# Sharing one buffer between the stages of a four-layer network, with image 1's norm inside image 0's heads and image 0's sampling positions in two halves

## The chip, the cores and the metric

The kernel runs on one NeuronCore of one Trainium2 chip, as one program. Its time is the device time of one execution in microseconds; the median of three runs is given. Everything is float32. TensorE is called PE here, its weight loads PEld, VectorE DVE, ScalarE ACT, GpSimd POOL; SP is the engine that issues most of the direct DMAs.

## The reference

Four images of 32 x 32 pixels and 384 channels go through four layers. Each layer is pre-normed (a group norm with 32 groups of 12 channels) and added back to its input.

```python
# layer 0: deformable attention, 6 groups = 6 heads of 64 channels
q = x @ w_q + b_q
o = conv3x3(q, w_off0, groups=6) + b_off0
o = gelu(layernorm(o) * ln_g + ln_b)
pos = tanh(o_group @ w_offp) * 16 + pixel              # one (x, y) per pixel and group
xs = bilinear_sample(x_group, pos)                     # four neighbours, weighted
k, v = xs @ w_k + b_k, xs @ w_v + b_v
bias = bilinear_sample(rpe_group, (pixel - pos) / 2)   # 1024 x 1024 a head
out = softmax(q k^T / 8 + bias) v;  x = x + out @ w_out + b_out

# layer 1: 12 heads of 32 channels
xg = x @ Wg + bg;  gc = depthwise_conv3x3_stride2(xg)
sim = sigmoid(l2norm(xg) l2norm(gc)^T);  gw = gamma * (sim sim^T) + 1 - gamma
attn = softmax(q k^T * scale) * gw;  attn = attn / attn.sum(queries);  x = x + (attn v) @ Wproj

# layer 2: local sums of x and x^2 over 5 columns and 20 channels, and their quotient
# layer 3: outlook attention, a 3 x 3 neighbourhood, weights from x @ Wa, values x @ Wv
```

## The kernel before

`Net` holds what is shared and two lanes. `Front` is layer 0 (tiles on the right side of SBUF), `Trunk` is layers 1 to 3 (tiles on the left). The Tile framework places tiles, decides a static order of instructions for each engine and inserts the waits; a few places are pinned in the order in which they are written. Engines and DMA queues work in order.

**Order of the whole.** The front of image 0 runs alone. From then on `Net.layer3` steps the trunk of image b as a generator; each step yields a weight, and the front of image b+1 is advanced by its own weights so that it stays a tenth ahead (TRUNK_STEPS 1109, FRONT_STEPS 714, LEAD 0.1). Image 3's trunk has no front beside it.

**PSUM.** `big` is a ring of two tiles of 128 x 1024, `bank` a ring of four of 128 x 512. The weights pool has three buffers.

**Front.** `inputs0` (L533) loads the image, transposes it (L545, copies by ACT), stores it to `x0`, norms it (statistics L306 and L307, group sums on PE L330, scaling L357), transposes the normed image back (L564) and writes it to memory in pairs of neighbouring pixels (L570), two DMAs for each of eight pixel blocks. Then come q (a `dense_t`, L376), the grouped convolution (L599), the layer norm (L628 to L650) and GELU (L654), and `positions` (L451), which makes sampling weights, the gather indices `sidx` (L509), and the bias windows' indices and fractions. For each of eight pixel blocks `gather` (L667) issues six indirect DMAs from POOL into one of three `gat` buffers, and `weigh` (L680 to L683) reduces it on DVE; a transpose (L694) and k and v follow.

**Heads of image 0.** `heads0` (L819) runs 96 blocks (6 heads x 2 halves of queries x 8 key blocks) in a pinned order, one block a turn. A block's bias window is gathered five blocks early (`win`, 8 buffers); ACT and DVE interpolate it in two steps each (`z`, 5 buffers, ACT L904 and DVE L885; then `lg`, 23 buffers, DVE L890), AHEAD = 8 turns before the block's logits are added (L935). Maximum, subtraction (L954), exponential and the products with v follow in later turns. Other images use `head0`, which does the same work (L752 to L808) as part of the front's steps.

**Trunk, layer 1.** `inputs1` (L1059) loads `x1`, norms it into another tile, multiplies by Wg, takes the stride-2 convolution on DVE (L1088, L1090), then `queries_keys` (L1096): for each of three channel blocks the q and k products go to a `big` tile each and to memory (`qd`, `kd`), from where `load_sums` and `load_pair` fetch them by head. `sums_step` (L1237), eight for each pair of heads, takes both `big` tiles: products (L1246), maxima (L1254) and exponentials with their sums (L1255). `hall` (L1158) spreads the inverse norms through a `big` tile and a bank. `sims` (L1276) makes the sigmoids (L1285, L1292). Then six `pair`s of heads: L1350, L1365, L1395, L1403 and L1404 are their group weights and products.

**Layer 3.** L1660 and L1662 write the outlook weights to memory and load them back as masks `mt`, half from the SP queue and half from the ACT queue; eight transposes of x (L1671) go to eight `y` tiles (L1675), L1683 multiplies masks and values, and each block is added and written out (L1692).

Of the kernel before, what the change touches and what calls it, by code (L numbers as in the profile page):

```python
# [19 lines left out]
I32 = mybir.dt.int32  # L20
# [52 lines left out]
class Net:  # L73


    def __init__(self, ctx, tc, a):
        self.tc, self.nc, self.a = tc, tc.nc, a
        nc = self.nc
        pool = lambda name, bufs, **kw: ctx.enter_context(
            tc.tile_pool(name=name, bufs=bufs, **kw)  # L80
        )
        self.const = pool("const", 1)
        self.wts = pool("wts", 3)
        self.ps2 = pool("ps2", 2, space=PSUM)
        self.ps1 = pool("ps1", 4, space=PSUM)
        self.dram = pool("dram", 1, space=DRAM)
        self.n = 0
        self.consts()
        self.scratch()
        self.front, self.trunk = Front(self, "right"), Trunk(self, "left")  # L90

# [102 lines left out]
    def scratch(self):  # L194
# [11 lines left out]

        self.k0 = dram("k0", [C, N])
# [72 lines left out]
class Lane:  # L280
# [33 lines left out]
    def norm(self, x, out, mv=None):  # L314


        nc = self.nc
# [4 lines left out]
        gmat = self.weights("gmat")  # L322
# [3 lines left out]
        def groups(src):  # L326
# [13 lines left out]
        nc.vector.tensor_scalar(mean, groups(mv[:, :, 0:1]), 1.0 / 12.0, None, ALU.mult)  # L340
# [8 lines left out]
        nc.scalar.activation(  # L349
            rstd, groups(d), AF.Sqrt, bias=self.eps[:, 0:1], scale=1.0 / 12.0  # L350
        )
        nc.vector.reciprocal(rstd, rstd)
        for k in range(KC):
            src = x[:, k, :]
            if len(out.shape) == 4:
                src = src.rearrange("p (y x) -> p y x", y=HW)
            nc.vector.tensor_scalar(  # L357
                out[:, k],
                src,
                mean[:, k : k + 1],  # L360
                rstd[:, k : k + 1],
                ALU.subtract,
                ALU.mult,
            )
# [34 lines left out]
class Front(Lane):  # L399
# [51 lines left out]
    def positions(self, oall):  # L451

        nc, v = self.nc, self.nc.vector
        NC = NJ * G
        tmp = self.wt([P, NC, GC], "a12", 2)
        og = oall.rearrange("p j (g c) -> p (j g) c", g=G)
        th = self.wt([P, 2, NC], "ix_th")
        for t in range(2):
# [6 lines left out]
        v.scalar_tensor_tensor(  # L465
            pos.rearrange("p t (j g) -> p (t j) g", g=G),
            th.rearrange("p t (j g) -> p (t j) g", g=G),
            HW / 2.0,
            bc(self.ref.rearrange("p t j -> p (t j)"), 2, G),
            ALU.mult,  # L470
            ALU.add,
        )
# [25 lines left out]
        w4 = self.wt([P, NC, 2, 2], "w4", 1)  # L498
        for lr in range(2):
            v.tensor_tensor(w4[:, :, lr, 0], wx[:, lr, :], one[:, 1, :], ALU.mult)  # L500
            v.tensor_tensor(w4[:, :, lr, 1], wx[:, lr, :], al[:, 1, :], ALU.mult)
        fi = self.wt([P, NJ, G], "ix_fi")
        fi2 = fi.rearrange("p j g -> p (j g)")
        sidx = self.wt([P, NC], "sidx", 1, I32)

        def index(out, hi, lo, mul, which):
            v.scalar_tensor_tensor(fi2, hi, float(mul), lo, ALU.mult, ALU.add)
            v.tensor_tensor(fi, fi, bc(self.gofs[:, which, :], 1, NJ), ALU.add)
            v.tensor_copy(out, fi2)  # L509

        index(sidx, fl[:, 1, :], fl[:, 0, :], HW, 0)
# [7 lines left out]
        f = self.f  # L519
# [7 lines left out]
        index(self.widx[:, 0], fl[:, 1, :], fl[:, 0, :], WROW, 1)  # L527

        v.tensor_scalar(fi2, fi2, float(HW // 2 * WROW), None, ALU.add)
        v.tensor_copy(self.widx[:, 1], fi2)  # L530
        return w4, sidx

    def inputs0(self, b):  # L533
        nc, v = self.nc, self.nc.vector
        pairs = self.pairs[b % 2]

        xin = self.wt([P, NJ, C], "a12", 2)
# [3 lines left out]
        x = self.wt([P, KC, N], "a12", 2)  # L541
        for j in range(NJ):
            ps = self.bank()
            for k in range(KC):
                nc.tensor.transpose(  # L545
                    ps[:, k * P : (k + 1) * P], xin[:, j, k * P : (k + 1) * P], self.ident
                )
            nc.scalar.copy(
                x[:, :, j * P : (j + 1) * P], ps[:, 0:C].rearrange("p (k n) -> p k n", k=KC)
            )  # L550
        nc.scalar.dma_start(self.x0[b % 2].rearrange("(k p) n -> p k n", p=P), x)
        xh = self.wt([P, KC, N], "a12", 2)
        self.norm(x, xh)
# [6 lines left out]
        pv = pairs.rearrange("(g s) (y c) -> y s g c", g=G, y=2)  # L560
        for j in range(NJ):
            ps = self.bank()
            for k in range(KC):
                nc.tensor.transpose(  # L564
                    ps[:, k * P : (k + 1) * P], xh[:, k, j * P : (j + 1) * P], self.ident
                )
            xn = self.wt([P, C], "xn", 2)
            nc.scalar.copy(xn, ps[:, 0:C])
            for y, first in ((0, HW + 1), (1, 1)):
# [3 lines left out]
                )  # L573

        yield 10
# [50 lines left out]
        for j in range(NJ):  # L626
            st = self.wt([P, 6], "ln_st", 2)
            v.bn_stats(st, oall[:, j, :])  # L628
            v.bn_aggr(mv[:, j, :], st)
        rstd = self.wt([P, NJ], "ln_rstd")  # L630
        nc.scalar.activation(
            rstd,
            mv[:, :, 1:2].rearrange("p j o -> p (j o)"),
            AF.Sqrt,
            bias=self.eps[:, 1:2],
        )
        v.reciprocal(rstd, rstd)
        for j in range(NJ):
            v.tensor_scalar(
                oall[:, j, :],  # L640
                oall[:, j, :],
                mv[:, j, 0:1],
                rstd[:, j : j + 1],
                ALU.subtract,
                ALU.mult,
            )
            v.tensor_tensor(
                oall[:, j, :], oall[:, j, :], self.rows[:, R_LNG : R_LNG + C], ALU.mult
            )
            v.tensor_tensor(  # L650
                oall[:, j, :], oall[:, j, :], self.rows[:, R_LNB : R_LNB + C], ALU.add
            )
        for j in range(NJ):
            nc.scalar.activation(oall[:, j, :], oall[:, j, :], AF.Gelu)  # L654
        yield 25
        w4, sidx = self.positions(oall)
        yield 20
# [161 lines left out]
    def heads0(self, work):  # L819
# [10 lines left out]
        AHEAD, SUB, OUT = 8, 10, 11  # L830
# [12 lines left out]
        def divide(step, k):  # L843
# [6 lines left out]
            elif step == 1:  # L850
# [3 lines left out]
                for q in range(2):  # L854
                    inv[q] = tile_of([P, HN], "lg", 23)
# [11 lines left out]
        def turn(t):  # L867
            i = t + AHEAD

            if i + 5 < n:  # L870
                h, q, j = blocks[i + 5]
                win[i + 5] = tile_of([P, (HH + 1) * WROW], "win", 8)
# [20 lines left out]
            if 0 <= i < n:  # L893
                lg[i] = tile_of([P, HN], "lg", 23)
# [6 lines left out]
            if 0 <= i + 1 < n:  # L901
                wv = win[i + 1].rearrange("p (r c) -> p r c", c=WROW)
                z[i + 1] = tile_of([P, HH, HW + 1], "z", 5)
# [88 lines left out]
        for i in range(4):  # L992
            h, q, j = blocks[i]
            win[i] = tile_of([P, (HH + 1) * WROW], "win", 8)
# [12 lines left out]
        self.load_keys(1)  # L1007
        for t in range(-3, n + OUT + 12):
            turn(t)
        yield 0  # L1010
# [25 lines left out]
class Trunk(Lane):  # L1036


    def image(self, b, out):
        with self.scope("l1y"):  # L1040
# [18 lines left out]
    def inputs1(self, b):  # L1059
        nc, v = self.nc, self.nc.vector  # L1060
        x = self.wt([P, KC, N], "x")
        for k in range(KC):
            nc.sync.dma_start(x[:, k, :], self.x1[b % 2][k * P : (k + 1) * P, :])
        xh = self.wt([P, KC, N], "xh")
        self.norm(x, xh)
        yield 15

# [28 lines left out]
        def queries_keys(ko):  # L1096
            for w, dst in ((wq, self.qd), (wk, self.kd)):
                ps = self.dense_t(w, xh, ko)
                t = self.wt([P, N], "qk", 2)
                if dst is self.qd:  # L1100
                    nc.scalar.mul(t, ps, HD1**-0.5)
                else:
                    v.tensor_copy(t, ps)
                nc.sync.dma_start(dst[ko * P : (ko + 1) * P, :], t)
# [9 lines left out]
        queries_keys(0)  # L1114
# [25 lines left out]
        queries_keys(1)  # L1140
        yield 14
        wv = self.weights("Wqkv", 2 * C)
# [4 lines left out]
        queries_keys(2)  # L1147
        yield 14
        self.sums_step(1, st)
        yield 10  # L1150
        values(range(NJ // 2))
        self.sums_step(2, st)
        yield 18
        for k in range(KC):
            rows, heads = slice(k * P, (k + 1) * P), slice(32 * k, 32 * k + 32)
            ps, pc = self.big(), self.bank()
            for out, lo in ((ps[:, 0:512], 0), (ps[:, 512:N], 512), (pc[:, 0:M1], N)):
                nc.tensor.matmul(  # L1158
                    out,
                    self.hall[heads, :],  # L1160
                    inv[heads, lo : lo + out.shape[-1]],
                    start=True,
                    stop=True,
                )
            t = self.wt([P, N + M1], "sq", 2)
            v.tensor_tensor(
                t[:, 0:N].rearrange("p (y x) -> p y x", y=HW),
                pads[k][:, 1:, 1:],
                ps.rearrange("p (y x) -> p y x", y=HW),
                ALU.mult,  # L1170
            )
            v.tensor_tensor(t[:, N:], raw[:, k, :], pc[:, 0:M1], ALU.mult)
# [4 lines left out]
            self.sums_step(3 + k, st)  # L1177
            yield 8
        for i in range(2):
            values(range(4 + 2 * i, 6 + 2 * i))  # L1180
            self.sums_step(6 + i, st)
        self.sums_finish(0, st)
        self.load_lse(0)
        yield 28
# [91 lines left out]
    def sims(self, p):  # L1276

        nc = self.nc
        sim = self.wt([P, 2, 2, N], "sim")
# [148 lines left out]
    def layers23(self, b, out):  # L1428
        with self.scope("l23"):
            self.x = self.wt([P, KC, N], "x")  # L1430
# [36 lines left out]
    def layer2(self):  # L1467
        nc, v = self.nc, self.nc.vector
        with self.scope("l2"):
# [8 lines left out]
            def squares(k):  # L1478
# [24 lines left out]
                d = self.wt([P, HW, HW], "d", KC)  # L1503
# [61 lines left out]
    def layer3(self, b, out):  # L1565
        nc, v = self.nc, self.nc.vector
        skew = self.skew[b % 2]
        with self.scope("l3"):
# [98 lines left out]
            ys = []  # L1667
            for i in range(NJ):
# [5 lines left out]
                y = self.wt([P, C], "y", NJ)  # L1674
                nc.scalar.copy(y, pt[:, 0:C])  # L1675
                ys.append(y)
            yield 20
            for i in range(NJ):
# [11 lines left out]
                y = ys[i]  # L1690
# [87 lines left out]
```

## Time and profile before

| | us |
|---|---|
| runs | 4781.11, 4804.75, 4805.06; median 4804.75 |
| profiled execution | 4803.82 |
| its span | 4802.0 |
| busy PE / DVE / ACT / POOL | 4201.4 / 3136.5 / 2411.3 / 942.6 |
| front 0 up to its k and v | 0 to 219 |
| heads of image 0 | 219 to 548 |
| trunk 0 with front 1 | from 574 |
| trunk 3 alone | 4030 to 4802 |

All times in the profile are microseconds from the start of the span. A row of the timeline gives start, duration, engine, source line, operation, destination and sources, shapes and count; in brackets stands the engine's idle time before it and what released it. A row of the groups gives busy time and mean ns of one, then the idle time before. In the lines of 40 digits, a digit is a busy share, or the granted TensorE clock, in tenths of one fortieth of the span. Float32 matmuls appear as two records each.

### The profile page before, as it was taken

The numbers are of one execution on the slowest core, as the hardware profiler recorded it, in microseconds if no ns is written. First come the engines' busy times: TensorE is split into PE (matmuls) and PEld (weight loads), VectorE is DVE, ScalarE is ACT, GpSimd is POOL, SyncE is SP. The second block draws the span as 40 slices with busy tenths as digits, with TensorE's granted clock in tenths as the row PEclk, the third lists the DMA queues.
The fourth block names the chain that finished last, engine by engine and source line by source line (L and its number), as shares of the span: only waits on it lengthen the run. The fifth ranks groups of instructions, "written<-read, shape, count | busy, mean of one in ns | idle before, by whom it ended". The sixth has DMA issues, their size and how long they took to land. (4 is left out here: it accounts for less than half of the span.)

```text
span 4802.0 us, 46610 instructions
## 1 busy us (share of the span) xinstructions
PE 4201.4 (87%) x15704; PEld 1793.1 (37%) x15704; DVE 3136.5 (65%) x5727; ACT 2411.3 (50%) x3693; POOL 942.6 (20%) x946
## 2 busy tenths in 40 slices
PE   5477798999999898899999989799999998999988
PEld 2222243333333353333333444343333334343444
DVE  3599655777877727577778744667686873455544
ACT  2166333666665313566767332456676631466642
POOL 0643104211212102311212110421121210000000
PEclk8689897999999987999999989799999998899998
DMA  6433234222212233321212133431121213201011
GB/s 118 142 102 103 81 101 131 84 60 57 71 40 73 75 116 123 106 57 48 80 50 68 44 100 116 130 98 55 38 77 39 79 47 109 86 25 31 19 39 40
DMA packets 230927, 366.82 MB, mean 76 GB/s; under 512 B 117475, under 2 KB 164672, under 8 KB 230688
## 3 DMA queue, kind: packets, MB, share of 16 engines
q1 hardware_dynamic: 169672, 197.36, 13.9%
q0 software_dynamic: 39936, 145.53, 10.3%
q10 hardware_dynamic: 21080, 20.96, 1.8%
q8 instruction: 124, 2.03, 0.2%
q14 instruction: 115, 0.94, 0.1%
HBM read 285.84 MB, written 78.21 MB: 76 GB/s over the span
## 5 line engine op out<-in xcount | busy, mean ns | idle before, releaser
L1404 DVE SCALAR_TENSOR_TENSOR e<-bank,gam,e 128x512 f32<-128x512 f32 x768 | 558.3, 749 | 571.8 <-ACT gn L1403 276.4
L1395 PE MATMUL bank<-sim,sg 128*128 128x512 f32 (+3 forms) x2304 | 877.4, 515 | 11.6 <-POOL sg L1350 8.9
L1255 ACT ACTIVATE big<-big,nmax 128x1024 f32<-128x1024 f32 x384 | 418.6, 1090 | 395.2 <-DVE nmax L1254 340.2
L1373 ACT ACTIVATE e<-big 128x1024 f32<-128x1024 f32 x384 | 376.9, 1019 | 363.4 <-PE big L1365 358.1
L1395 PEld LDWEIGHTS bank<-sim,sg 128*128 128x128 f32 x2304 | 408.3, 200 | 390.5 <-issue 301.4
L1254 DVE TENSOR_REDUCE nmax<-big 128x1 f32<-128x1024 f32 x384 | 453.5, 1218 | 77.0 <-PE big L1246 34.1
L752 POOL DMA_INDIRECT win<-strips,widx x288 | 308.1, 1070 | 629.2 <-DVE z L765 328.1
L1350 POOL TENSOR_SCALAR sg<-sim,gam 128x512 f32<-128x512 f32 x192 | 148.5, 776 | 1430.8 <-PE bank L1395 1140.7
L1365 PE MATMUL big<-qa,ka 64*128 64x512 f32 x1536 | 414.1, 630 | 14.8 <-ACT big L1255 8.8
L1246 PE MATMUL big<-k,q 32*128 32x512 f32 x1536 | 355.2, 697 | 81.4 <-ACT big L1255 38.2
L667 POOL DMA_INDIRECT gat<-pairs,sidx x192 | 210.1, 1094 | 500.6 <-DVE ix_gt L479 401.7
L773 PE MATMUL bank<-qpad,kz 128*128 128x512 f32 x576 | 283.0, 617 | 15.0 <-DVE e L1404 15.0
L808 PE MATMUL bank<-lg,va 128*64 128x512 f32 x576 | 265.0, 602 | 16.3 <-ACT lg L806 16.2
L808 PE MATMUL bank<-lg,ones 128*64 128x512 f32 x576 | 264.3, 602 | 0.0
L770 DVE SCALAR_TENSOR_TENSOR lg<-z,bias_f,lg 128x512 f32<-128x512 f32 x288 | 227.9, 803 | 40.1 <-ACT lg L769 38.6
L764 ACT ACTIVATE z<-win,bias_f 128x528 f32<-128x528 f32 x288 | 207.1, 739 | 63.3 <-DVE lg L770 39.2
L1365 PEld LDWEIGHTS big<-qa,ka 64*128 64x128 f32 x1536 | 135.5, 189 | 272.4 <-issue 159.3
L765 DVE SCALAR_TENSOR_TENSOR z<-win,bias_f,z 128x528 f32<-128x528 f32 x288 | 216.2, 769 | 27.0 <-DMA win<-strips,widx 16.6
L805 DVE TENSOR_TENSOR lg<-lg,tb 128x512 f32<-128x512 f32 x288 | 187.6, 705 | 51.4 <-ACT tb L798 51.4
L1339 PE MATMUL bank<-e,vs 128*32 128x512 f32 x1536 | 210.9, 605 | 2.1 <-DVE vs L1333 2.1
L769 ACT ACTIVATE lg<-z,bias_f 128x512 f32<-128x512 f32 x288 | 201.4, 720 | 19.1 <-PE bank L808 10.7
L376 PE MATMUL big<-xh,w 128*128 128x512 f32 x432 | 199.3, 619 | 12.2 <-ACT big L1255 10.8
(291 smaller groups left out, 6658.3 us busy)
## 6 DMA issues: line engine op xcount, KB each, us to landing
pairs<-xn SPq DMA_DIRECT2D x64, 192.0 KB
q<-qd SPq DMA_DIRECT2D x48, 256.0 KB
w<-in_gmat SPq DMA_DIRECT2D x16, 576.0 KB
w<-in_w_off SPq DMA_DIRECT2D x12, 576.0 KB
w<-in_Wqkv SPq DMA_DIRECT2D x12, 576.0 KB
a<-in_x SPq DMA_DIRECT2D x16, 384.0 KB
x<-a ACTq DMA_DIRECT2D x4, 1536.0 KB
win<-strips,widx POOLq DMA_INDIRECT x384
```

Source lines behind the costliest of these rows:

```text
L752: nc.gpsimd.indirect_dma_start(out=win, out_offset=None, in_=self.strips[:, :], in_offset=bass.IndirectOffsetOnAxis(ap=self.widx[:, q, c : ...
L765: v.scalar_tensor_tensor(z, wv[:, 1 : HH + 1, 0 : HW + 1], sc(0, 1), z, ALU.mult, ALU.add)
L770: v.scalar_tensor_tensor(lg, z[:, :, 1 : HW + 1], sc(0, 0), lg, ALU.mult, ALU.add)
L773: nc.tensor.matmul(ps, kz[:, j * P : (j + 1) * P], both, start=True, stop=True)
L808: nc.tensor.matmul(po[out, :], w, lf, start=j == 0, stop=j == NJ - 1)
L1246: nc.tensor.matmul(ps[r][:, h * 512 : (h + 1) * 512], self.q4[rows, i * P : (i + 1) * P], self.k4[rows, 0:512], start=True, stop=True,)
L1254: v.tensor_reduce(nmax[:, r, i : i + 1], ps[r], AX.X, ALU.max, negate=True)
L1255: nc.scalar.activation(ps[r], ps[r], AF.Exp, bias=nmax[:, r, i : i + 1], accum_out=den[:, r, i : i + 1],)
L1365: nc.tensor.matmul(ps[:, r, :], ka[rows, j * P : (j + 1) * P], qa[rows, cols], start=True, stop=True,)
L1373: nc.scalar.activation(e, ps, AF.Exp)
L1395: nc.tensor.matmul(ps[:, (mid - i0) * P :], sg[:, r, m, :], sim[:, r, m, mid * P : i1 * P], start=m == 0, stop=m == 1,)
L1404: v.scalar_tensor_tensor(e[:, r, :], ps, self.gam[:, 1:2], e[:, r, :], ALU.add, ALU.mult, accum_out=tot[:, r, h : h + 1],)
```

## The change

The amount of arithmetic stays nearly as it was; what moves is when it is done and where its results lie.

1. A pool `keep` on the trunk's side holds one tile `whole` of 128 x 4096. By turns it is the next image's x (normed in place), the `sim` of a pair, and the x of layers 2 and 3 with a spare quarter. `Trunk.start` loads the next image's x in layer 3, ahead of the output products.
2. In `inputs1` the q and k products go to two banks each, one product after every sums step; `hall` works in banks; the values are spread out.
3. In `layer3` the transposed x goes to one tile under the tag of the norm's output, which the values read until then.
4. `normed` is split from `inputs0`. For image 1 it runs inside `heads0`, one step a turn from turn 17 on, and leaves the normed image in memory (`xh1`), from where `inputs0` loads it. In exchange the rings of `heads0` are smaller.
5. The layer norm uses two fused operations instead of three, and for image 0 norm and positions are done in two halves of the pixel blocks.

```diff
+        self.trunk.work = self.trunk.keep = pool("keep", 1, side="left")
...
     def norm_steps(self, x, out, mv=None, gmat=None):        # norm, with a yield between its steps
...
+    def early0(self):
+        with self.scope("l0p"):
+            xh = yield from self.normed(1)
+            self.nc.sync.dma_start(self.xh1.rearrange("(k p) n -> p k n", p=P), xh)
...
+        if b == 1:
+            xh = self.wt([P, KC, N], "a12", 2)
+            nc.sync.dma_start(xh, self.xh1.rearrange("(k p) n -> p k n", p=P))
+            yield 25
+        else:
+            xh = yield from self.normed(b)
...
+        parts = 2 if b == 0 else 1
+        size = NJ // parts
+        for part in range(parts):
+            js = range(size * part, size * (part + 1))
...
+            for i, j in enumerate(js):
+                o = oall[:, j, :]
+                v.scalar_tensor_tensor(
+                    o, o, mv[:, j, 0:1], self.rows[:, R_LNG : R_LNG + C], ALU.subtract, ALU.mult)
+                v.scalar_tensor_tensor(
+                    o, o, rstd[:, i : i + 1], self.rows[:, R_LNB : R_LNB + C], ALU.mult, ALU.add)
+            for j in js:
+                nc.scalar.activation(oall[:, j, :], oall[:, j, :], AF.Gelu)
+            yield 25 / parts
+            self.positions(oall, js, tmp, w4, sidx)
+            yield 20 / parts
...
-        AHEAD, SUB, OUT = 8, 10, 11
+        AHEAD, SUB, OUT = 5, 10, 11        # lg 23 -> 20, win 8 -> 6, z 5 -> 4
...
+        other = self.early0()
         for t in range(-3, n + OUT + 12):
             turn(t)
+            if t > 2 * NJ:
+                next(other, None)
...
+    def start(self, b):
+        x = self.whole()[1]
+        for k in range(KC):
+            self.nc.sync.dma_start(x[:, k, :], self.x1[b % 2][k * P : (k + 1) * P, :])
+        self.begun = x, self.weights("gmat")
...
     def image(self, b, out):
+        if b == 0:
+            self.start(b)
+        x, gmat = self.begun
+        self.norm(x, x, None, gmat)
+        self.xh = x
+        yield 15
...
-        def queries_keys(ko):
-            for w, dst in ((wq, self.qd), (wk, self.kd)):
-                ps = self.dense_t(w, xh, ko)
+        def product(w, ko, dst):
+            t = self.wt([P, N], "qk", 2)
+            for h in range(2):
+                ps, out = self.bank(), t[:, h * 512 : (h + 1) * 512]
...
-        queries_keys(0)
+        product(wq, 0, self.qd)
+        product(wk, 0, self.kd)
...
-        queries_keys(1)
+        product(wq, 1, self.qd)
...
         self.sums_step(0, st)
-        queries_keys(2)
+        product(wk, 1, self.kd)
         yield 14
         self.sums_step(1, st)
-        values(range(NJ // 2))
+        product(wq, 2, self.qd)
+        yield 14
         self.sums_step(2, st)
+        product(wk, 2, self.kd)
         for k in range(KC):
+            self.sums_step(3 + k, st)
...
-            ps, pc = self.big(), self.bank()
+                ps = self.bank()[:, 0:n]           # hall, in three parts
...
+            values(range(k, k + 1))
...
-        sim = self.wt([P, 2, 2, N], "sim")
+        sim = self.whole()[0].rearrange("p (r m n) -> p r m n", r=2, m=2)
...
-                d = self.wt([P, HW, HW], "d", KC)
+                d = self.wt([P, HW, HW], "d", 2) if k < 2 else self.spare
...
-            ys = []
+            ys = self.wt([P, KC, N], "xh").rearrange("p k (a c) -> p (k a) c", c=P)
+            ys = ys.rearrange("p (i k) c -> p i (k c)", k=KC)
             for i in range(NJ):
...
-                y = self.wt([P, C], "y", NJ)
-                nc.scalar.copy(y, pt[:, 0:C])
+                nc.scalar.copy(ys[:, i], pt[:, 0:C])
             yield 20
+            if b + 1 < NB:
+                self.start(b + 1)
             for i in range(NJ):
```

## The prediction

> **What bounds the kernel now.** I read the page first: busy shares, then the 40 slices.
>
> ```profile
> PE 4201.4 (87%) x15704; PEld 1793.1 (37%) x15704; DVE 3136.5 (65%) x5727; ACT 2411.3 (50%) x3693; POOL 942.6 (20%) x946
> PE   5477798999999898899999989799999998999988
> PEclk8689897999999987999999989799999998899998
> ```
>
> TensorE is the bound over the whole, with 600.6 us idle. The slices say where: one is 120 us, and the first five hold 4 to 7 tenths (front 0 alone, then its heads); the others below 9 lie at image changes. The change adds and removes hardly any arithmetic, so only these places can move. Next the windows (columns: length, then busy of PE, PEld, DVE, ACT, POOL, then granted clock, DMA share, GB/s): the heads, and the sums stretch of image 0.
>
> ```profile
> 300.00:400.00 100.00, 74.81 (x208) 21.13 (x204) 99.10 (x152) 65.58 (x103) 40.64 (x34) 0.91 0.36 105
> 740.00:760.00 20.00, 17.59 (x37) 7.30 (x37) 15.09 (x16) 7.30 (x13) 15.73 (x15) 0.50 0.56 178
> 760.00:780.00 20.00, 10.56 (x40) 5.23 (x40) 6.52 (x7) 5.95 (x11) 11.87 (x12) 0.76 0.64 183
> ```
>
> The heads are VectorE's (99%): work put on VectorE there costs its full time, work on PE or ACT has room. The sums stretch belongs to no engine: it is a chain. Last the timeline and the groups by form, for single steps.
>
> ```profile
> 119.62 1.22 POOL L667 DMA_INDIRECT gat<-pairs,sidx  x1 [100.74 <-DVE ix_gt L479]
> 121.15 0.95 POOL L667 DMA_INDIRECT gat<-pairs,sidx  x1 [0.30 <-issue]
> 132.46 0.90 PE L694 MATMUL bank<-ident,xn 128*128 128x128 f32 x3 [46.68 <-DVE xn L683]
> L460 DVE TENSOR_TENSOR a<-a,rows 128x3072 f32<-128x3072 f32 x2 | 6.7, 3358 | 0.7 <-ACT a L654 0.6
> L639 DVE TENSOR_SCALAR a<-a,ln_mv,ln_rstd 128x384 f32<-128x384 f32 x8 | 3.5, 476 | 0.1
> L306 DVE BATCH_NORM_STATS2 gn_st<-a 128x6 f32<-128x512 f32 x6 | 3.7, 678 | 0.0
> L357 DVE TENSOR_SCALAR a<-a,gn_mean,gn_rstd 128x1024 f32<-128x1024 f32 x3 | 2.3, 809 | 0.0
> ```
>
> ```profile
> 591.37 4.26 PE L545 MATMUL bank<-ident,a 128*128 128x128 f32 x24
> 598.35 3.12 PE L330 MATMUL bank<-gn_mv,w 128*128 128x1 f32 x14 [2.73 <-DVE gn_mv L307]
> 627.36 23.41 PE L599 MATMUL big<-qpad,w 64*64 64x512 f32 x216
> 657.38 0.41 DVE L1088 TENSOR_SCALAR raw<-xp,cols 128x256 f32<-128x256 f32 x1 [49.06 <-ACT xp L1076]
> 716.70 0.19 DVE L509 CAST sidx<-ix_fi 128x48 int32<-128x48 f32 x1
> 779.46 2.15 PE L1285 MATMUL big<-xg,gc 64*128 64x512 f32 x4 [9.44 <-ACT big L1255]
> 785.98 2.22 POOL L667 DMA_INDIRECT gat<-pairs,sidx  x1 [10.77 <-DMA qa<-lse]
> 800.14 0.75 DVE L1404 SCALAR_TENSOR_TENSOR e<-bank,gam,e 128x512 f32<-128x512 f32 x1 [7.67 <-ACT gn L1403]
> 1738.07 1.12 ACT L580 ACTIVATE qpad<-big,cols 128x1024 f32<-128x1024 f32 x1 [12.08 <-DMA mt<-skew]
> 1782.22 0.55 PE L330 MATMUL bank<-gn_mv,w 128*128 128x1 f32 x2 [4.25 <-issue]
> 4036.39 0.56 PE L330 MATMUL bank<-gn_mv,w 128*128 128x1 f32 x2 [8.85 <-DMA x<-x]
> ```
>
> Read in pairs: 591.37 to 627.36 is front 1's norm standing ahead of its convolution while VectorE idles 49 us; 657.38 to 800.14 is the sums stretch; the last two are PE waiting for the next image's x.
>
> **Sampling positions in halves (image 0).** The gathers start when `sidx` exists (119.3) and run POOL-bound, 48 in 66.4 us, 1.384 each. By the code the first half should need half of the wide work. In the compiled program's order, though, VectorE does the second half's norm, and three of its four wide operations, ahead of the first half's index. From 83.7 on: 8 statistics pairs 5.7 (0.553+0.178 each), 16 norm operations at 0.47 (row L639) 7.5 where 24 took 10.7, 7 half-size wide ones at 1.69 (half of 3.36) 11.8, small ones 4, two more table loads on ACT 1 to 2: about 31, so `sidx` near 114, 5 earlier. Against it, three window gathers now stand among the 48 on POOL: 3 x 1.38 = 4.1. Net -1 (bounds +3, -5).
>
> **Heads 0.** AHEAD 8 to 5: three blocks' two interpolation steps (0.766 + 0.745) move from VectorE's idle time at k, v into the 99% stretch: +4.5. Image 1's norm on VectorE: 6 statistics 3.7, 3 aggregates 0.6, small ones 0.8, 3 scalings 2.3: +7.4, all open. On PE 48 transposes, 8.9 (24 took 4.26 and 4.6), lie in 25 us idle per 100; on ACT 16 copies at 0.48 and two table loads, 10, lie in 34 per 100; on SP 16 pair writes, about 1 us each to issue, stand ahead of key loads that are issued 18 turns (62 us) early. If ACT's cover fails it costs 10. The norm is a chain VectorE-PE-VectorE-PE-ACT-VectorE, and VectorE, in order, waits wherever a link is late, with the whole next turn queued behind it: not shown in this stage, 0 to 10 by the gaps of the same norm later (2.73, 0.93, 1.50); one step a turn of 3.4 us covers most, so I take 1.5. The smaller rings keep the window's lead of 5 turns (17 us; a gather lands 2 us after issue): nothing. Heads and start together **+12.4** (+5 to +20).
>
> **Start of the merged phase.** PE had 36.0 us from 591.37 to 627.36. Remaining is the q product, 36 records at 0.43 = 15.5; the transposes and waits go: **-20.5** (-14 to -22). The normed image comes back from memory instead of the raw one, the same 1.5 MB, so that is hidden as before. What is late next is trunk 0's own norm, unchanged.
>
> **Sums stretch, images 0 to 2.** From the first convolution tap to the first L1404: 142.7, 148.9, 143.2 us. `sidx` came at +59.3, and then 48 gathers of 1.25 to 1.38 should need 60 to 66; they stopped at 775 to 786 because the weighing that frees their three buffers stood on VectorE behind the sums, and the sums waited for the two `big` buffers that products and norms also used. After: products and `hall` in banks, one sums step after each product. Shorter LN, no wait for bigs: `sidx` at +53.5; gathers 66.5; the tail after the last gather 4.8 as before; waits for weighing 3. Sum 128. Gains 14.7, 20.9, 15.2 = **-50.8**. Against: q and k come back through memory 8 to 10 us after their product instead of 26, so PE may stand 5 to 10 there, with sums, products and values queued behind. Bounds: -15 (that wait, and the old chain nearly whole) to -75 (gathers 60 and no waits).
> Here the clock matters. PE is 88% busy in 740 to 760 and is granted 0.50.
> The Trainium skill (TensorE: Matmul & The Clock Gate, A second HAM failure mode: psum-queue depth-cycling) says that work cycling through PSUM banks idles PE so often that the gate closes and reopens; that speaks against banks. By it, 117.8 us of matmul in this stretch at 0.81 would be 191 at 0.50, 48 over the stretch; with that three times in place of -50.8 the sum would be an estimated +114. No row before shows products in banks.
> I take the clock as it was: the low grants stand beside the waits that go.
>
> **Image 3's sums** have no front beside them: 113.2 us, with 14 us of VectorE waiting before the first L1404. I take **-9** (0 to -13).
>
> **Boundaries.** The next x is loaded after the first output write instead of after all eight: the 4.25 us wait goes, and with it some of the clock of 0.57 in the 20 us behind, some 3. Against it, outputs now live in one tile free only after the values, so their transposes fill no gap; ACT's copies stand behind its four mask loads (ACT idle 12.08 up to 1738), and PE meets the outputs' products before q and convolution that it ran at 1732.7: +4. Each -3, two of them **-6** (-14 to +6). The third, without a front: 8.85 waited, **-8** (-4 to -12). The last image's end waits for its masks: **+1** (to +4).
>
> Sum: 12.4 - 20.5 - 50.8 - 9 - 6 - 8 + 1 = -80.9. The profiled execution took 4803.82 (span 4802.0), 0.9 under the median of 4804.75, so both bases agree: 4722.9, say **4723**. All upper ends together give +20 - 14 - 15 - 0 + 6 - 4 + 4 = -3, all lower ones over -130; taken together such ends are unlikely, so the forecast's own range is 4680 to 4790.
>
> **Rivals.** *The stretch keeps its length.* The chain is then the memory round trip and VectorE's order, not the bigs. For it: VectorE's 105 busy of 143. Against: it idles 9 us for a big at 766 to 777. Then 12.4 - 20.5 - 6 - 8 + 1 = -21: 4783.
> *Slower: the heads lose their lead.* With 5 blocks ahead and the norm's copies on ACT, the two ACT steps of a block (0.74 + 0.72, rows L764 and L769) lie open before VectorE's each turn: 96 x 1.46 = 140, so 4723 + 140 = 4863. It decides from 0.85 us a turn (81/96) and shows as slower from 1.1. For it: 99.1% leaves no slack. Against: ACT is 66% busy, and five turns are 17 us for 1.46 of work.
> *The halves do what they say.* If VectorE finished the first half alone, 15 us sooner and not 5, and the window gathers stayed behind, front 0 would give 14 more: 4709. Against: the compiled order.
>
> **How the numbers follow.** Forecast 0.62; stretch unchanged 0.15, split 0.06 under and 0.09 over the bound of 0.5% (24 us, about what can be told from no change); heads slower 0.16; halves 0.04; small sums of bad ends 0.03, within the bound. Faster 0.62 + 0.06 + 0.04 = 0.72, same 0.09 + 0.03 = 0.12, slower 0.16. The range 4680 to 4828 leaves out the slower rival (0.16) and 0.04 below.
>
> **What would show it.** Convolution of front 1 starting 16 us after trunk 0's last norm product, not 36; stretches of about 128; no wait for x at the boundaries; heads 0 longer by 12 with VectorE still at 99%; gathers of image 0 ending near 185. It is wrong if VectorE falls under 95% in the heads, if PE shows new gaps behind q and k, or if the stretches stay above 140.

## The result, and the profile after

The changed kernel took 4731.30 us (median of four runs, 4728.61 to 4736.50), the kernel before 4799.59 us beside it: a ratio of 0.9863, 95% interval 0.9840 to 0.9887. The forecast was 4723 of a base of 4804; by the two profiled executions the gain was 4803.82 - 4731.65 = 72.2 us, forecast 80.9; by the two medians it was 68.3.

The page after: the busy times, the 40 slices and the granted clock.

```profile
PE 4165.4 (88%) x15704; PEld 1776.1 (38%) x15704; DVE 3133.8 (66%) x5772; ACT 2416.1 (51%) x3711; POOL 945.7 (20%) x946
PE   5477788999999988899899989899999999999988
PEclk8688888999999988999999989899999998999998
```

The matmul records are as many as before and busy 36.0 us less, and idle time on PE fell from 600.6 to 564.4, by 36.2. So by the records, whose ends are modelled, half of the gain is matmul that lasts less long. The granted clock is a tenth lower in slices 4 and 6, in image 0's heads and at front 1's convolution, and a tenth higher in slices 7, 16, 26 and 35, which lie over the sums stretches of the four images. This window lies in image 0's heads (columns as before):

```profile
300.00:400.00 100.00, 80.40 (x253) 29.26 (x251) 94.00 (x152) 64.49 (x106) 35.78 (x30) 0.85 0.60 172
```

152 VectorE instructions as before, but 94.0 us busy and not 99.1: some of the 152 are the norm's short ones, and VectorE waits. The prediction had named under 95% as a sign of being wrong; over the whole of these heads VectorE is busy 324.7 of 337.3 us, 96%. The waits of VectorE in the heads after (what, total, times, longest) say for what:

```profile
DVE gn_mean L350 <- PE bank L338: 3.3, 1, 3.3
DVE z L925 <- ACT z L944: 3.1, 6, 0.8
DVE gn_rstd L363 <- ACT gn_rstd L361: 1.3, 1, 1.3
```

The timeline rows that answer to those shown of before:

```profile
112.23 1.16 POOL L707 DMA_INDIRECT gat<-pairs,sidx  x1 [93.48 <-DVE ix_fl L492]
601.55 18.20 PE L388 MATMUL big<-a,w 128*128 128x512 f32 x36
619.68 23.41 PE L637 MATMUL big<-qpad,w 64*64 64x512 f32 x216
649.74 0.41 DVE L1146 TENSOR_SCALAR raw<-xp,cols 128x256 f32<-128x256 f32 x1 [45.24 <-issue]
703.79 0.19 DVE L521 CAST sidx<-ix_fi 128x48 int32<-128x48 f32 x1
740.32 1.22 DVE L1322 TENSOR_REDUCE nmax<-big 128x1 f32<-128x1024 f32 x1 [9.23 <-issue]
774.02 2.22 POOL L707 DMA_INDIRECT gat<-pairs,sidx  x1 [5.92 <-DVE xn L723]
789.24 0.75 DVE L1472 SCALAR_TENSOR_TENSOR e<-bank,gam,e 128x512 f32<-128x512 f32 x1 [8.49 <-ACT gn L1471]
1770.07 1.62 PE L338 MATMUL bank<-gn_mv,w 128*128 128x1 f32 x14
3983.19 1.62 PE L338 MATMUL bank<-gn_mv,w 128*128 128x1 f32 x14
```

The gathers of image 0 start 7.4 us earlier. Front 1's convolution follows directly on its q product. The last two rows have no wait in brackets: x is there when the norm wants it. In the sums stretch the index comes at 703.79 - 649.74 = +54.1 us (it was +59.3), but the stretch is still 139.5 us long, with a wait of 9.23 on VectorE that nothing in the profile releases. PE also has a new wait, 5.9 us in each of images 0 to 2, for the copy of a k product out of its bank (its row at 702.25, L1160, waits for VectorE's L1170). Adding the two traces up by stage:

| from, to | before | after | gain | forecast |
|---|---|---|---|---|
| start to last v block of image 0 | 220.0 | 215.5 | 4.5 | 1.0 |
| heads of image 0, to the last subtraction | 323.1 | 337.3 | -14.2 | -13.4 |
| layer 0's output of image 0 | 31.3 | 32.6 | -1.3 | 0 |
| to front 1's convolution | 53.0 | 34.3 | 18.7 | 20.5 |
| sums stretches, images 0 to 2 | 142.8, 148.9, 143.2 | 139.5, 135.9, 132.6 | 26.9 | 50.8 |
| sums stretch, image 3 | 113.2 | 95.8 | 17.4 | 9 |
| pairs, layers 2 and 3 and image change, three times | 1006.0, 1007.9, 949.4 | 1001.2, 997.0, 944.0 | 21.1 | 14 |
| end | 633.3 | 634.2 | -0.9 | -1 |

Fronts and sums stretches are measured as in the prediction: a stretch runs from the first convolution tap to the first L1404 (now L1472).

### The profile page after: what moved, and what is told of

It is laid out like the page before. It is cut to its first block, busy times and chain, and to the rows that moved or that the text cites. A ratio compares the mean times of both kernels' runs of the same rounds, so it can differ in the third digit from the quotient of the medians.

```text
span 4729.8 us, 46690 instructions
## 1 busy us (share of the span) xinstructions
PE 4165.4 (88%) x15704; PEld 1776.1 (38%) x15704; DVE 3133.8 (66%) x5772; ACT 2416.1 (51%) x3711; POOL 945.7 (20%) x946
## 5 line engine op out<-in xcount | busy, mean ns | idle before, releaser
L1472 DVE SCALAR_TENSOR_TENSOR e<-bank,gam,e 128x512 f32<-128x512 f32 x768 | 558.4, 749 | 573.0 <-ACT gn L1471 276.8
L1463 PE MATMUL bank<-whole,sg 128*128 128x512 f32 (+3 forms) x2304 | 873.2, 513 | 2.5 <-DVE e L1472 2.5
L1463 PEld LDWEIGHTS bank<-whole,sg 128*128 128x128 f32 x2304 | 406.5, 199 | 379.9 <-issue 301.7
L1418 POOL TENSOR_SCALAR sg<-whole,gam 128x512 f32<-128x512 f32 x192 | 147.1, 769 | 1399.4 <-PE bank L1463 1139.5
L1433 PE MATMUL big<-qa,ka 64*128 64x512 f32 x1536 | 411.7, 627 | 14.7 <-ACT big L1323 8.9
L1314 PE MATMUL big<-k,q 32*128 32x512 f32 x1536 | 327.2, 690 | 74.7 <-ACT e L1441 35.3
L1433 PEld LDWEIGHTS big<-qa,ka 64*128 64x128 f32 x1536 | 134.7, 187 | 270.4 <-issue 153.9
L814 DVE TENSOR_TENSOR lg<-bank,lg 128x512 f32<-128x512 f32 x288 | 192.4, 684 | 20.7 <-PE bank L813 18.4
```

Source lines behind the costliest of these rows:

```text
L1314: nc.tensor.matmul(ps[r][:, h * 512 : (h + 1) * 512], self.q4[rows, i * P : (i + 1) * P], self.k4[rows, 0:512], start=True, stop=True,)
L1433: nc.tensor.matmul(ps[:, r, :], ka[rows, j * P : (j + 1) * P], qa[rows, cols], start=True, stop=True,)
L1463: nc.tensor.matmul(ps[:, (mid - i0) * P :], sg[:, r, m, :], sim[:, r, m, mid * P : i1 * P], start=m == 0, stop=m == 1,)
L1472: v.scalar_tensor_tensor(e[:, r, :], ps, self.gam[:, 1:2], e[:, r, :], ALU.add, ALU.mult, accum_out=tot[:, r, h : h + 1],)
```

## The experiments

These ran on three chips, and chips differ: the kernel before took 4797.4 us beside the first four runs, 4767.8 beside the next four and 4800.5 beside the last. Only kernels of one chip are compared by time; marks inside a trace are compared where the chip is the same.

**The control.** 

> The changed kernel again, as the control beside which the next three are read. All theories: 4728 to 4737 us, as in its first four runs; heads of image 0 from the last v block to the last subtraction 337 us, sums stretches near 139.5, 136.0, 132.6 and 95.8 us, front 1's convolution 34 us after the end of layer 0's output of image 0.

4733.1 us, ratio 0.9862 (0.9841 to 0.9883); heads 338.1, stretches 140.4, 139.7, 132.6 and 95.8.

**Image 1's norm out of the heads.**

```diff
-        other = self.early0()
...
-            if t > 2 * NJ:
-                next(other, None)
...
-        if b == 1:
+        if False:
```

> Image 1's norm goes back from the heads to the start of the merged phase; the smaller rings stay. Theory (terms of the prediction, with the chain's waits as the new trace has them, 4.9 us): the heads shrink by 7.9 us of VectorE work and 4.9 us of waits, from 337 to 324; the convolution of front 1 comes 53 us after layer 0's output and not 34, so +19; net +6, 4737. Rival A (the norm in the heads costs more than its own work, by its DMA traffic and PE work): heads fall to 318 or less, net 0 or below, 4731 or less. Rival B (norm is hidden in the heads): heads stay above 333, net +15 or more, 4746.

4739.6 us, ratio 0.9874 (0.9852 to 0.9895). By time it is within the intervals; the marks of the two traces separate it: heads 328.2 against 338.1, the convolution 52.1 us after layer 0's output against 34.0. So the norm in the heads costs 9.9 and brings 18.1. The forecast had 8.9 (7.4 of work, 1.5 of waits) and 20.5; of the 9.9, VectorE is busy for 6.2 and idle for 3.7 (324.7 busy of 338.1 against 318.5 of 328.2). These heads are still 5 us longer than those of before (323.1, and 324.0 in a later run on another chip). The smaller AHEAD was forecast at 4.5 of that, and the traces hold what it counts: 93 and 95 of VectorE's two interpolation steps stand in the heads, where before had 90 and 92.

**The positions in one part.** `parts = 1`.

> Image 0's sampling positions in one part. Theory of the prediction (halves are worth 1 us, since three window gathers stand in the gather queue): k and v of image 0 end 1 us later, total +1. What the new trace suggests: the first index came 7.3 us earlier and k and v ended 4.5 earlier, of which the fused layer norm is some 2.5 us by itself; so +2 to +3, 4734. Rival (the halves do what they say): +5 to +14, k and v end after 220 us.

4733.4 us, ratio 0.9858 (0.9835 to 0.9881): no difference from the control, and k and v end at 216.1 against 215.5. The halves are worth 0.6 us at k and v. The first gather starts at 115.1, four later than the control's 111.1, but no window gathers stand among them, and the last ends at 180.9 against 180.5. The rival fell, and so did the guess of 2 to 3.

**The old order of the sums, in banks.**

```diff
         product(wq, 1, self.qd)
+        product(wk, 1, self.kd)
...
         self.sums_step(0, st)
-        product(wk, 1, self.kd)
-        yield 14
+        product(wq, 2, self.qd)
+        product(wk, 2, self.kd)
...
+        values(range(NJ // 2))
```

> Products, hall and values keep their banks, but stand in the order of before (all q and k products early, values in two blocks). Theory (banks free the two large buffers, which is what the stretch waited for): at most a third of the gain goes, the four stretches grow by 15 together, 4746. Rival (the gain is the interleaving: one product or value block between two sums steps): all of it goes, 44 us over four stretches, 4775. Third: order costs nothing, 4731.

4766.7 us, ratio 0.9932 (0.9911 to 0.9953), 33.5 over the control: between the theory (15) and its rival (44). Stretches 146.9, 142.9, 144.4, as in the kernel before (142.8 to 148.9 in its two traces), and 104.2. Banks alone gain nothing in images 0 to 2 and 9 us in image 3. In the old order, then, the large buffers were not what the stretches of images 0 to 2 waited for.

**The new order, in the large buffers.**

```diff
+            whole = self.big()
             for h in range(2):
-                ps, out = self.bank(), t[:, h * 512 : (h + 1) * 512]
+                ps, out = whole[:, h * 512 : (h + 1) * 512], t[:, h * 512 : (h + 1) * 512]
...
+            both = self.big()
             for at, n, src, out in parts:
-                ps = self.bank()[:, 0:n]
+                ps = both[:, at : at + n] if at < N else self.bank()[:, 0:n]
```

> The new order of the sums stretch, but q and k products and the inverse norms' spread in the two large buffers as before. Read against the control (stretches 140.4, 139.7, 132.6, together 412.7, and 95.8; 4733). Theory, from the run with the old order in banks (434.2 and 104.2): order carries the gain of images 0 to 2 and banks give 9 in image 3 alone; so 405 to 418 and 104, 4742. Rival, the prediction's step (the sums waited for the large buffers): 430 or more and 110, 4765.

4797.9 us, ratio 1.0055 (1.0038 to 1.0071): slower than the kernel before on that chip. Stretches 152.0, 152.1, 146.2 and 123.8, where the changed order in banks has 125.7, 125.7, 125.3 and 95.8 on the same chip (the run with the late x, below). The theory, order alone, falls by 21 to 28 us a stretch; for the new order the prediction's step, that the sums wait for the large buffers, stands. The waits of VectorE in image 0's stretch here, and then with banks:

```profile
DVE sq L1241 <- PE big L1236: 17.3, 5, 4.2
DVE nmax L1324 <- PE big L1316: 8.8, 3, 5.8
DVE qk L1171 <- PE big L1161: 7.8, 2, 4.7
```

```profile
DVE nmax L1322 <- PE big L1314: 3.0, 2, 1.6
DVE qk L1170 <- PE bank L1160: 2.9, 2, 1.5
```

33.9 us against 5.9. Interleaving puts every product between two sums steps, which need both large buffers; so in images 0 to 2 the order pays only with banks, and banks pay only with the order. The two stretches as windows, large buffers first (columns as before):

```profile
647.85:799.85 152.00, 129.03 (x315) 50.49 (x315) 102.20 (x165) 61.05 (x97) 50.23 (x50) 0.80 0.41 126
648.86:774.52 125.66, 107.90 (x314) 44.77 (x314) 102.37 (x165) 60.56 (x97) 54.85 (x50) 0.89 0.49 153
```

Of the 26.3 us between them 21.1 are PE's records lasting longer, at a granted clock of 0.80 and not 0.89, and 5.2 are idle time of PE.

**Three value blocks earlier.**

```diff
-            values(range(k, k + 1))
+            values(range(2 * k, 2 * k + 2))
...
-            values(range(3 + i, 4 + i))
+            values(range(6 + i, 7 + i))
...
-        values(range(5, NJ))
```

> The last three value blocks (18 matmul records, 6.0 us) leave the end of the sums stretch: two blocks after each of three sums steps, one after each of the last two. Theory (the stretch ends with a chain of 22 us from the last exponential of the sums over their logarithm, the values and the sigmoids, with or without a front): each stretch loses 4 to 6, image 3's among them, 4733 - 20 = 4713. Rival (the gathers on POOL, before the first product's scaling, end the stretch): only image 3 gains, 4 to 6, 4728.

4710.8 us, ratio 0.9884 (0.9868 to 0.9901), some 9 us slower than the run with the late x on the same chip. Image 3 gained 1.1 and the others lost 4.2 to 5.1 each: both expectations missed. The sigmoids were ready 5.6 us earlier (115.5 after the stretch's start against 121.1), and the gathers ended where they had (122.2 against 122.3). PE then stood waiting for POOL. The first products after the gathers, here and with the values late:

```profile
768.68 3.78 PE L1462 MATMUL bank<-whole,sg 128*128 128x512 f32 x4 [7.45 <-POOL sg L1417]
```

```profile
771.95 3.70 PE L1463 MATMUL bank<-whole,sg 128*128 128x512 f32 x8 [0.32 <-POOL sg L1418]
```

After 7.45 us of waiting four records took what eight took without; the clock granted in the two rows is 0.50 and 1.00. The Trainium skill (TensorE: Matmul & The Clock Gate, HAM oscillation) says that an idle gap above about 3.4 us closes the clock gate to half; these rows agree. So the gathers end the stretch, the rival's mechanism. The slower clock is not all that the edit cost. From the last gather to the first L1471 or L1472 image 0 has 7.8 us here and 3.4 with the values late; the first group weights were copied out 1.8 us later, and the other 2.6 are a wait for the pair's exponential, whose logits the compiled order now puts behind the products that wait for POOL (L1432 at 772.39), where they stood ahead of them (L1433 at 769.41). Images 1 and 2 show the same order.

**The next x loaded late, twice.** The first attempt moved the load in the source only, behind the output loop.

> The next image's x is loaded after all eight output writes again, and nothing else is undone. Theory from the two traces (from the last output product to the next first convolution tap 32.6, 32.2, 28.0 before and 20.3, 20.3, 16.7 now): those 12 us come back at each of three image changes, +36, 4769. The prediction's terms (a wait of 4.25 and 3 of clock, twice, and 8.85): +23, 4756. Rival (the early load is hidden by the front's convolution anyway): +9 or less, from the change without a front alone, 4742.

The compiled order of SP still has it after the first output write. 4701.5 us, ratio 0.9863 (0.9846 to 0.9879), and image changes of 20.2, 20.3 and 16.7 us: it tells nothing of the load, and serves as control of its chip. The second attempt forces it:

```diff
             for i in range(NJ):
...
                 nc.sync.dma_start(out[i * P : (i + 1) * P, :], y)
                 yield 4
+            if b + 1 < NB:
+                hold = self.wt([P, 1], "hold")
+                v.tensor_tensor(hold, ys[:, NJ - 1, 0:1], self.x[:, 0, 0:1], ALU.add)
+                self.start(b + 1)
```

> The next image's x is held back for good: one 128 x 1 addition on VectorE that needs the last output block and the old x keeps the shared tile busy until all outputs are added (0.15 us of work; the earlier attempt to move the load left the compiled order as it was). Theory from the traces (from the last output product to the next first tap 32.6, 32.2, 28.0 before and 20.3, 20.3, 16.7 now): about 12 us come back at each of three image changes, +36. The prediction's terms (4.25 and 3 twice, 8.85): +23. Rival (it is hidden by the front's convolution): only the change without a front loses, +9 to +12.

4754.4 us, ratio 0.9908 (0.9887 to 0.9929). The control by its ratio would be 0.9862 x 4800.45 = 4734.2 here, so +20, with some 10 either way by the intervals. From the last output product to the next tap 29.4, 29.6 and 24.5 against 20.3, 20.3 and 16.7: 9.1, 9.3 and 7.8, in all 26. That is nearest to the prediction's terms (23); the full 36 is not the load's alone.

**Heads with 2 blocks ahead.** `AHEAD = 2`.

> Bias windows of image 0's heads interpolated 2 blocks ahead and not 5, rings unchanged. Theory (the prediction's term: each block less ahead moves 1.51 us of VectorE work into the heads): heads 338 to 342.6, +4.5, 4738. Rival (the slower one of the prediction: with too little lead the two ACT steps of a block, 1.46 us, lie open each turn): heads up to 478, +140, 4870; anything over 350 speaks for it.

4699.1 us, ratio 0.9853 (0.9836 to 0.9869); heads 338.0 against 337.4 on the same chip. The slower rival of the prediction is dead: even with two blocks ahead the heads grow by 0.6 and not by 140. The expected +4.5 was missed too, since it was counted wrongly: with AHEAD 5 only 3 z and 1 lg steps are done by the last v block, with AHEAD 2 one and none. That is 2 x 0.766 + 0.745 = 2.3, of which 0.6 shows.

**The norm in the heads with more room.**

```diff
         sums = groups(mv[:, :, 0:1])
         yield
-        nc.vector.tensor_scalar(mean, sums, 1.0 / 12.0, None, ALU.mult)
+        yield
+        yield
+        pin(nc.vector.tensor_scalar(mean, sums, 1.0 / 12.0, None, ALU.mult))
...
         yield
-        nc.vector.reciprocal(rstd, rstd)
+        yield
+        pin(nc.vector.reciprocal(rstd, rstd))
```

> Image 1's norm in the heads takes four more turns, and its mean and reciprocal are pinned two turns after the products that they need, so that VectorE does not stand for them. Theory (VectorE stood 3.3 us for the mean and 1.3 us for the reciprocal in the heads of the changed kernel, with the next turn queued behind): heads 337.5 to 333, total -4.5. Rival (VectorE only waits later in the turn): heads stay at 337, total 0.

4735.5 us, ratio 0.9858 (0.9829 to 0.9886), heads 337.5: the rival. VectorE's waits in these heads:

```profile
DVE z L930 <- ACT z L949: 7.4, 7, 3.4
DVE lg L999 <- ACT tb L994: 1.3, 1, 1.3
```

The waits for mean and reciprocal are gone, and as much came back as a wait for ACT. ACT stood for the norm too: from 300 to 400 us it waited 5.1 us for the transposed blocks, 4.3 of them at once, and loaded two tables around the square root:

```profile
342.03 1.28 ACT L365 ACT_TABLE_LOAD   x1
343.33 0.26 ACT L365 ACTIVATE gn_rstd<-bank,eps 128x3 f32<-128x3 f32 x1
343.61 1.28 ACT L1000 ACT_TABLE_LOAD   x1
```

The norm is a chain through three engines, and here moving one link moved the wait.

**The layer norm unfused.**

```diff
-                v.scalar_tensor_tensor(
-                    o, o, mv[:, j, 0:1], self.rows[:, R_LNG : R_LNG + C], ALU.subtract, ALU.mult)
-                v.scalar_tensor_tensor(
-                    o, o, rstd[:, i : i + 1], self.rows[:, R_LNB : R_LNB + C], ALU.mult, ALU.add)
+                v.tensor_scalar(o, o, mv[:, j, 0:1], rstd[:, i : i + 1], ALU.subtract, ALU.mult)
+                v.tensor_tensor(o, o, self.rows[:, R_LNG : R_LNG + C], ALU.mult)
+                v.tensor_tensor(o, o, self.rows[:, R_LNB : R_LNB + C], ALU.add)
```

> The layer norm in three operations as before (8 more on VectorE for each image, and 0.4 us more a pixel block). Theory (the gathers end the sums stretch, and start when the index exists): the index of images 1 to 3 comes 3 us later, from +54.1 to +57, and each of three stretches grows by as much; front 0's k and v end 1 to 2 us later; total +10. Rival (the chain of sums ends the stretch): the index comes later and the stretches do not change, +1.

4744.1 us, ratio 0.9889 (0.9855 to 0.9923), beside 4735.5 of the run with the spread norm. The index comes at +57.3, 3.2 later, as expected; the stretches are 134.2, 141.9 and 143.4, in sum 419.5, beside 420.1 of that run on this chip. They vary from image to image by more than the effect, so it is inconclusive.

**The kernel before, for its trace.**

> The kernel before, for its trace on the chip of the next three runs: chips differ (the kernel before took 4797 on one and 4768 on another, and the same sums stretches of the changed kernel 138 and 125.5 us). No theory in dispute; if this chip is like the first, the sums stretches are 143, 149, 143 and 113 again; if like the second, the theory that the waits without a visible cause belong to the chip expects 130 to 135 in images 0 to 2 and 113 in image 3.

4811.6 us in its one run; stretches 145.3, 147.0, 143.9 and 115.7. This chip is like the first: the runs beside it, with the changed order in banks, have 132.6 to 143.4 in images 0 to 2. So the kernel before has no trace on the chip where the stretches last 125.5, and what they gain there is open.

## Why the prediction was right

**The sum and its signs held, in part by luck.** Each term that was not put at nothing has the sign that was forecast. The total came 8.7 us short in the profiled executions. The sums stretches of images 0 to 2 fell 23.9 short, the other terms fell 3.8 short together, and front 0, image 3 and the boundaries gave 3.5, 8.4 and 7.1 more than forecast: misses in different stages cancel. Of the prediction's own signs, the convolution after 18 us (16), no wait for x and gathers of image 0 ending at 181.6 (185) held. VectorE at 94.0% in the window shown and the new wait behind k are signs that it had named for being wrong. The stretches lie at its limit of 140: 139.5, 135.9 and 132.6, and 140.4 for image 0 in the control.

**Front 0.** Forecast -1 with bounds of +3 and -5; measured -4.5. The reading of the compiled order was right: with halves the gathers start earlier and end hardly earlier, because window gathers stand among them (0.6 us at k and v). The first index came at 111.8, forecast near 114, although one price was too low: the fused norm operations last 0.60 us, where the row L639 (0.476) was taken. They read a second whole tile, as the row L647 (0.553) does, which was the nearer one.

**Heads.** +14.2 against +13.4 (4.5 + 7.4 + 1.5). The norm's share is 9.9; its waits were undersized (1.5 taken of bounds 0 to 10, where 4.9 stand at its links in the trace and 3.7 are left of them in the stage's length), and they were not had back by moving VectorE's links.

**Start of the merged phase.** 18.7 against 20.5: the q product of 36 records took 18.2 us and not 15.5. The clock granted in these 18.2 us was 0.86, and 15.5 / 0.86 = 18.0; they stand behind the waits of trunk 0's norm.

**Sums stretch: the mis-sized term.** Forecast 128 us each and 50.8 in sum, measured 139.5, 135.9, 132.6 and 26.9. The index came at +54.1 (forecast +53.5). The gathers end the stretch (the earlier values). The prediction's account of the wait before is only half borne out: with the new order the large buffers are the wait (152 us with them), with the old order they are not (the run with the old order in banks). What was mis-sized is the 3 us of waits for weighing: POOL stood 14.2, 8.4 and 4.7 us for weighings that free its buffers, so that the gathers took 79.4, 75.8 and 72.4, and without these waits 65.2 to 67.7, where 66.5 was forecast. On the second chip the same code (the run with the late x) has gathers of 67.8, 67.8 and 67.0 with no such wait above 0.3, and stretches of 125.7, 125.7 and 125.3, which is near the forecast's 128. Why the weighings are late on the other chips is not shown. What stands ahead of them there are waits without a releaser. In image 0 at the same place, the run with the late x on that chip and then the control:

```profile
730.43 2.36 DVE L1322 TENSOR_REDUCE nmax<-big 128x1 f32<-128x1024 f32 x2 [1.59 <-PE big L1314]
```

```profile
731.52 0.69 DVE L1239 TENSOR_TENSOR sq<-xp,bank 128x512 f32<-128x512 f32 x1 [1.41 <-remote]
743.60 1.23 DVE L1322 TENSOR_REDUCE nmax<-big 128x1 f32<-128x1024 f32 x1 [11.39 <-issue]
```

In the control the products for this maximum ended at 732.6 by the records, and the maximum started 11 us later. Such a wait stood in before already:

```profile
776.88 2.36 DVE L1254 TENSOR_REDUCE nmax<-big 128x1 f32<-128x1024 f32 x2 [9.59 <-issue]
```

The products for this one (L1246) ended at 770.02. PE's 9.44 us at 779.46 is its consequence, since ACT's exponential waited for the maximum, and PE for the exponential. The prediction read the 9.59 as VectorE idling "for a big", which no row says, and the change left it as it was (9.23 at 740.32). Nor do the gathers end every such stretch: with x held back, image 1's gathers took 67.9 and ended 10.2 us before the stretch did, behind a wait of PE of 7.5 us without a releaser.

**The clock.** The prediction took the clock as it was, and from the Trainium skill (TensorE: Matmul & The Clock Gate, A second HAM failure mode: psum-queue depth-cycling), which tells of a bf16 kernel whose clock swings while it cycles through PSUM banks, it worked out an estimated +114, at half the clock throughout. In the float32 runs here banks had the higher clock: the new order was granted 0.89 in banks and 0.80 in the large buffers. (Products in banks were not new either: the values, L390, had them before.) But the clock did not stay as it was. In the four stretches 0.81, 0.77, 0.80 and 0.86 became 0.82, 0.85, 0.86 and 0.98. PE's records there, as many as before within two, last 28.5 us less in all (460.6 to 432.1 us busy), which is the larger part of the 44.3 gained. The sum had no term for this.

**Image 3.** 17.4 against 9, outside the bounds of 0 to 13: with no gathers, banks (9 us in the run with the old order) and interleaving (8.4 more) both count in full. The 14 us wait that the term was read from was only a part of what they remove: PE's records there last 12.0 us less (clock 0.86 to 0.98), and its idle time fell by 5.4.

**Boundaries.** 21.1 in sum against 14; the load of x is worth 20 to 26 by itself. The +4 charged for masks and outputs was about right: layer 3 and what precedes it grew by 7.6, 1.1 and 6.0, while the image changes shrank by 12.4, 12.0 and 11.4.

**The rivals.** The stretch that keeps its length came half true by size (half of the gain did not come), and for another cause. The slower one is excluded. The halves did not do what they say.

## What to carry to other kernels

Before an edit is called a gain, look at the compiled order of each engine: it decided that the halves of the positions bring 0.6 us, and it undid a move of a load in the source. When two edits share a buffer ring, price them together: with the old buffers the interleaved order was 21 to 28 us a stretch slower than with the new ones, the new buffers alone gave nothing in three stretches of four, and both together gave the gain. Look at the granted clock of a stage as well as at its waits: in the sums stretches matmul that lasted less long was worth more (28.5 us) than the waits that went (15.8). Work moved into a stage bound by one engine cost its own time there and, as a chain over several engines, more than half as much again in waits (6.2 us busy and 3.7 idle, against 18.1 gained).

## What the runs showed of the hardware that was not expected

**Waits without a releaser were longest on two of three chips, beside the gathers.** In the sums stretches of images 0 to 2, with the changed order in banks, PE stood without a releaser that the profile shows for 0.8 to 15.4 us a stretch on the first and third chip (control 3.8, 7.5, 2.2; with x held back 11.7, 15.3, 10.2) and for 0.0 in the three such runs on the second (late x in the source, 2 blocks ahead, earlier values). In image 3, without gathers, it is 0.0 in all of them. It is not tied to gathers alone: the old order has 2.7 us in image 3, on two chips, and the large buffers 1.6 on the second chip. The kernel before was 30 us faster on the second chip as well. The cause is open: no run separates the gathers' DMA traffic from their descriptors, and which chip is given cannot be chosen.

**A maximum follows its matmul late, by the records.** Where these waits are long, PE's records have ended 7 to 11 us before VectorE, which reads PSUM, starts (770.02 to 776.88 in before, 732.6 to 743.60 in the control); since matmul ends in the profile are modelled, it may be that PE itself was late. That was not tried.
